# Row-mode steps of two attention stages split into single products, dealt over four row groups, with another queue rule in the planner's model

## The chip, the core and the metric

One core of a Trainium2 chip runs the whole program. The metric is device time in microseconds (us) of one execution, as the median of the runs. The engines are named as in the profile: PE is the matrix engine, DVE the vector engine, ACT the scalar engine, POOL the general one, SP the one that issues most DMAs.

## The reference, cut to what matters

Two layers are applied to `x` of 2 x 2048 tokens with 256 features. Each adds a product of two branches to `x`:

```python
x = L0_attn_x
xn = _layernorm(x, axis=-1)
s = _L0_attn_ref(xn, ...)            # linear attention (elu features), 16 heads of 16
g = _silu(_L0_ffn_ref(xn, ...))      # a block: causal softmax attention, then 8 experts, top 2
x = x + s * g
xn = _layernorm(x, axis=-1)
s = _L1_attn_ref(xn, ...)            # causal softmax attention, 16 heads of 16 + 16
g = _silu(_L1_ffn_ref(xn, ...))      # a product with an int4-rounded matrix, plus a low-rank term
x = x + s * g
```

Both softmax attentions, of 16 heads over 2048 tokens and two batches, are

```python
scores = where(causal, q @ k.T / scale, far below zero)
probs = softmax(scores, axis=-1)
out = probs @ v
```

## The kernel before, in words

The program has three stages: the softmax attention of layer 0 together with the linear attention and the routing of tokens to experts (0 to about 1400 us of the profile), the experts (to about 1930 us), and the softmax attention of layer 1 with everything around it. The change touches the first and the last, which share `run_attention`.

**Groups and rounds.** Heads are handled four at a time, so there are 8 groups (2 batches x 4). A head's queries and keys lie on 32 partitions, so a score product contracts over 32 rows only, and four of them, for the four heads, can stream through PE's four row groups side by side. This is called *row mode* here; in *column mode* (`on="col"`) four products with 32 output columns each run side by side, and in mode *all* one product uses the whole array. `run_attention` makes a list of rounds (`u`). One round holds

- **pass A** of one (query tile `t`, key block `k`): for each of the four heads `j` one product of 128 queries by up to 512 keys (L575), heads 0 and 1 into a pair of PSUM banks, heads 2 and 3 into another; DVE then takes the row maximum of each pair (L594). In layer 0, a block on the diagonal gets a mask first, added by four small bf16 products for each head (`hide`, L534); in layer 1 DVE adds it (L588);
- **pass B** of one (query block `c` of 256, key pair `p`): for each head two products (L609) that give keys by queries into one bank, and ACT's exponential of it (L621). On the diagonal, four bf16 products for each head add the mask (`hide_pair`, L541). In layer 1, one or two bf16 products with three rows subtract the maximum (`less_maximum`, L1697, L1698, L1700); in layer 0 it sits in a spare row of the queries.

Round by round, pass A runs ahead of pass B. With full key blocks, a head has one product of 512 columns and two of 256 in a round. Sums of probabilities with values (L911, L1740) follow in column mode, and projections, transposes, routing and linear attention lie between rounds in modes *all* and *col*.

**The order of the products in a round** is written out by hand. In the loop `for i in (0, 2)` the products come in these groups: A of head 0, B of head 2 (both products), A of head 1, B of head 3; then the masks of A for head 0 (four) and head 1 (four), then those of B for head 2 and head 3; and for `i = 2` the same with A of heads 2 and 3 and B of heads 0 and 1. Each line of this list is one planner step of strand `S`, and PE keeps the order of a strand.

**The planner** (`Plan`) decides the rest: where between the rounds each other step lies on each engine, and which of 8 PSUM banks it takes. `advance` plays the program with costs given in each `S(...)` call, picks the step that can start first (with a handicap for each strand), and `run` searches over jittered handicaps with a beam of 8. Steps of other strands on PE are let in only where the next `S` step opens a round, or where the next `S` step would wait more than `PATIENCE` = 0.3 us longer, mostly for a bank. What the planner sets is only the order of instructions on each engine; the chip then runs each engine's list with semaphores. In the model before, a row step may be sent 0.01 us after the one before it, however many are still waiting for the same group, and it pays a weight load of `LOAD["row"]` = 0.105 us if its group was idle:

```python
                if s.row:
                    if t > groups[s.on] or st.cold[s.on]:
                        t += s.load
                    st.cold[s.on] = False
...
                done, free["PE"] = t + s.cost + self.TAIL - self.GAP, sent + 0.01
```

An f32 product is two records in the trace, each with a weight load (LDWEIGHTS) and a matmul; a bf16 product is one.

Of the kernel before, what the change touches and what calls it, by code (L numbers as in the profile page):

```python
# [17 lines left out]
P = 128  # L18
# [76 lines left out]
class State:  # L95


    def __init__(self, plan):
        self.main = next(iter(plan.queues.get(("S", "PE"), ())), None)
        self.can = {k: q[0] for k, q in plan.queues.items() if not q[0].before}  # L100
        self.waits = [s.before + (s is not plan.queues[s.key][0]) for s in plan.steps]
        self.ready = [0.0] * len(plan.steps)
        self.slot = [None] * len(plan.bufs)
        self.left = [b.uses for b in plan.bufs]
        self.until = [0.0] * len(plan.bufs)
        self.guest = [None] * len(plan.bufs)
        self.since = {k: [0.0] * (plan.BANKS if k == "s" else len(x)) for k, x in plan.kinds.items()}
        self.free, self.groups, self.cold = {}, [0.0] * 4, [True] * 4
        self.mode, self.used, self.held = None, 0.0, {}
        self.todo, self.done, self.value = len(plan.steps), [], 0.0  # L110

# [9 lines left out]
class Plan:  # L121
# [100 lines left out]

    def advance(self, st, handicaps, until):

        free, groups, can, ready = st.free, st.groups, st.can, st.ready
        while st.todo:
            best = shut = None
            low = low_shut = 1e30
# [2 lines left out]
            for key, s in can.items():  # L231
                strand, eng = key
                t = ready[s.n]
                x = free.get(eng, 0.0)
                if x > t:
                    t = x
                busy, closed = t, False
                if eng == "PE":
                    closed = strand != "S" and not (gap and st.used + s.cost <= self.LIMIT)
                    x = top if s.kind != st.mode else groups[s.on] if s.row else top - self.MODE  # L240
                    if x > busy:
                        busy = x
                later = 0.0 if closed else handicaps.get(strand, 0.0)
                if busy + later >= (low_shut if closed else low):
                    continue
                take = ()
                if any(st.slot[b.n] is None for b in s.bufs):
                    found = self.places(st, strand, s, t)
                    if not found:
                        continue  # L250
                    t, take = found
                    if t > busy:
                        busy = t
                if closed:
                    if busy < low_shut:
                        low_shut, shut = busy, (busy, busy, key, s, take, t)
                elif busy + later < low:
                    low = busy + later
                    best = (low, busy, key, s, take, t)
# [4 lines left out]
            _, t, key, s, take, sent = best  # L264
# [18 lines left out]
            done = t + s.cost  # L283
            free[s.eng] = done - min(self.OVERLAP.get(s.eng, 0.0), 0.7 * s.cost)
            worth = self.WORTH[s.eng] * s.cost
            if s.eng == "PE":
                st.used = st.used + s.cost if key[0] != "S" else 0.0
                kind = s.kind
                if kind != st.mode:
                    if kind == "row":  # L290
                        groups[:] = [max(t, x) for x in groups]
                    st.cold[:] = [True] * 4
                if s.row:
                    if t > groups[s.on] or st.cold[s.on]:
                        t += s.load
                    st.cold[s.on] = False
                elif t > max(groups) or st.cold[0]:
                    t += s.load
                    st.cold[0] = False
                done, free["PE"] = t + s.cost + self.TAIL - self.GAP, sent + 0.01  # L300
                if kind == "row":
                    st.mode, groups[s.on] = "row", t + s.cost
                    worth /= 4
                else:
                    st.mode, groups[:] = s.on, [t + s.cost] * 4
            elif s.eng == "SP":
                free["SP"] = t + 0.06
            st.value += worth
# [69 lines left out]
def kernel(ctx: ExitStack, tc: tile.TileContext, i: dict, out: bass.AP):  # L378
    nc = tc.nc
# [45 lines left out]
    cols = keep.tile([P, 8], F32, name="cols")  # L425
# [31 lines left out]
    QC = 256  # L457


    def t_row(n):  # L460
        return 0.00167 * n
# [62 lines left out]
    LAG = 1  # L524
    SUM_LAG0, SUM_LAG = 1, 2
    PREP_AT = 14
    T_HIDE_A, T_HIDE_B = 0.15, 0.28

    def hide(out, j, mask):

        r = slice(32 * j, 32 * j + 32)
        for q in range(4):
            cols = slice(32 * q, P)
            nc.tensor.matmul(out[:, cols], ident_h[r, q], mask[r, q, cols], start=False, stop=q == 3)  # L534

    def hide_pair(out, j, mask):

        r, v = slice(32 * j, 32 * j + 32), out.rearrange("p (n k) -> p n k", n=2)
        for q in (3, 2, 1, 0):
            cols = slice(0, 32 * q + 32)  # L540
            nc.tensor.matmul(v[:, :, cols], ident_h[r, q], mask[r, q, :, cols], start=False, stop=q == 0)  # L541

    def halves_of(c, p):

# [5 lines left out]
    def run_attention(plan, make, prepare, subtract, sum_keys, finish, last_sum, before=None, others=(), between=False, causal=None):  # L550
# [6 lines left out]
        S = plan.step  # L557
# [10 lines left out]
        def pass_a(g, t, k, i, w, mx, parts):  # L568
# [9 lines left out]
                )  # L578

            def products(x):  # L580
                return S("S", "PE", t_row(w), lambda: score(x), r=[(g.qt, t), *((g.kt, n) for n in keys)], w=[(s, x)], on=i + x)

            def rest():
                for x in range(2) if diagonal and causal is None else ():
                    S("S", "PE", T_HIDE_A, lambda x=x: hide(s.t[:, x, w - P : w], i + x, mask_q), r=[(s, x), "ident_h", "mask_q"], w=[(s, x)], on=i + x)
                if diagonal and causal is not None:
                    for x in range(2):
                        S("A", "DVE", t_dve(w) + 0.07, lambda x=x: nc.vector.tensor_tensor_reduce(  # L588
# [12 lines left out]
        def pass_b(g, c, p, j, pt):  # L601
# [2 lines left out]
            w = P + QC if diagonal else 2 * QC  # L604
            ahead = before is not None and p > 0

            def score():
                for n, (kj, q0, at) in enumerate(halves_of(c, p)):
                    nc.tensor.matmul(  # L609
                        s.t[:, at], g.kt.t[r, kj * P : (kj + 1) * P], g.qt.t[r, QC * c + q0 : QC * (c + 1)],  # L610
                        start=n == 0 and not ahead, stop=n == 1 and not (diagonal or before and not ahead),
                    )

            def rest():
                if before and not ahead:
                    S("S", "PE", 0.25 * t_row(w), before(g, c, j, s, diagonal, False, not diagonal), r=[s, g.mh[c]], w=[s], on=j, load=0.026)
                if diagonal:
                    S("S", "PE", T_HIDE_B, lambda: hide_pair(s.t[:, : 2 * P], j, mask_h), r=[s, "mask_h"], w=[s], on=j)

            def weigh():  # L620
                S("B", "ACT", t_act(w), lambda: nc.scalar.activation(pt.t[:, j, :w], s.t[:, :w], AF.Exp, scale=0.25), r=[s], w=[(pt, j)])  # L621

            reads = [(g.kt, 2 * p), (g.kt, 2 * p + 1), (g.qt, 2 * c), (g.qt, 2 * c + 1)]
            opener = None
            if ahead:
                opener = S("S", "PE", 0.25 * t_row(w), before(g, c, j, s, diagonal, True, False), r=[g.mh[c]], w=[s], on=j, load=0.026)
                reads.append(s)
            step = S("S", "PE", t_row(w), score, r=reads, w=[s], on=j)
            return opener or step, rest, weigh

        for part in prepare(groups[0]):
            part()
# [1 line left out]
        for u in range(at + last_sum + 1):  # L634
# [7 lines left out]
            if b:  # L642
                gb, cb, p = b
                pt = Buf("pt")
            first = None
            for i in (0, 2):


                more = []
                if a:  # L650
                    products, after_a = pass_a(g, t, k, i, wa, mx, parts)
                for x in range(2):
                    if a:
                        plan.pace = products(x)
                        first = first or plan.pace
                    if b:
                        step, rest, weigh = pass_b(gb, cb, p, (i + 2 + x) % 4, pt)
                        first = first or step
                        more.append((rest, weigh))
                if a:  # L660
                    after_a()
                for rest, _ in more:
                    rest()
                for _, weigh in more:
                    weigh()
            for call in late:
                call()
            if first and opens:
# [845 lines left out]
    with ExitStack() as sc:  # L1514
# [176 lines left out]
        def less_maximum(G, c, j, s, diagonal, first, last):  # L1691
            r = slice(32 * j, 32 * j + 3)

            def product():
                m = G.mh[c].t[r]
                if diagonal:
                    nc.tensor.matmul(s.t[:, :P], ones_h[r], m[:, P:], start=first, stop=False)  # L1697
                    nc.tensor.matmul(s.t[:, P : P + QC], ones_h[r], m, start=False, stop=last)  # L1698
                else:
                    nc.tensor.matmul(  # L1700
                        s.t.rearrange("p (n q) -> p n q", n=2), ones_h[r], m[:, None].to_broadcast([3, 2, QC]),
                        start=first, stop=last,
                    )

            return product

        def sum_keys(G, c, pair, last):

# [173 lines left out]
```

## Time and profile before

| | |
|---|---|
| median of 3 runs | 3334.01 us (3331.4 to 3335.59) |
| the profiled execution | 3333.86 us; its span in the trace 3332.1 us |
| granted PE clock, mean | 0.982 |
| PE, DVE, ACT, POOL busy | 3205.3, 2132.9, 1623.4, 1620.8 us |
| row-mode records of L575, L609 | 5120 (2560 products), 9216 (4608 products) |
| mask records of L534, L541 | 2048, 2048 |

The span is 1.8 us shorter than the execution's time, and that time is within 0.2 us of the median, so differences in the trace can be read as differences in the median. The start of a matmul in the trace is when its weights begin to load if its group was idle, so a first product looks longer than the next; ends are modelled. Two records of the same row group that follow each other without a gap show by their starts how long one streams.

### The profile page before, as it was taken

The page shows a single profiled execution, that of the slowest core. Times are in us where ns is not written, and L with a number is a line of the kernel's source. Part 1 is how long each engine was busy: PE and PEld are TensorE (multiplying, and loading weights), DVE is VectorE, ACT ScalarE, POOL GpSimd, SP SyncE. Part 2 cuts the span into 40 slices and gives each one's busy share as a digit, 9 for nine tenths or more (in the row PEclk, how much of TensorE's full clock was granted, in tenths as well). Part 3 has the DMA queues.
Part 4 walks back from the last instruction along what each step waited for, and adds up shares of the span by engine and source line. Part 5 has one row for each costly group of instructions (what it writes and reads, how often), then busy time and mean ns, then how long its engine had stood idle before and what let it go on. Part 6 is the DMA issues. An engine that isn't in the chain of part 4 may idle for free.

```text
span 3332.1 us, 92022 instructions
## 1 busy us (share of the span) xinstructions
PE 3205.3 (96%) x39748; PEld 2271.7 (68%) x39748; DVE 2132.9 (64%) x4250; ACT 1623.4 (49%) x3264; POOL 1620.8 (49%) x2006
## 2 busy tenths in 40 slices
PE   7999999989999999979999989999999999999998
PEld 5677777767777776656666646666766666767775
DVE  5677677667777767641112057787777776777785
ACT  3565555555555555511112155555554555544554
POOL 5442222333233222310000057898987776878887
PEclk9999999999999999989999989999999999999999
DMA  5000000000000010133342131110101001000000
GB/s 198 2 2 2 5 8 8 17 30 26 6 11 5 9 45 13 49 109 115 109 131 94 64 105 43 38 43 29 39 17 33 27 17 40 23 12 23 14 29 24
DMA packets 99742, 134.51 MB, mean 40 GB/s; under 512 B 9461, under 2 KB 76739, under 8 KB 99334
## 3 DMA queue, kind: packets, MB, share of 16 engines
q1 hardware_dynamic: 93190, 114.74, 10.6%
q0 software_dynamic: 6144, 13.88, 1.3%
q8 instruction: 311, 5.10, 0.6%
q14 instruction: 97, 0.79, 0.1%
HBM read 93.75 MB, written 37.75 MB: 39 GB/s over the span
## 4 chain that ended last, share of the span: by engine, by line
PE 50%; DVE 3%; POOL 2%; ACT 1%; issue 1%; DMA 0%; POOLq 0%; another core or an unknown queue 0%; SPq 0%; DVEq 0%; ACTq 0%
PE banks L575 9%; PE banks L609 8%; PE banks L414 8%; PE banks L1740 7%; PE s L1488 7%; PE s L1494 7%; PE banks L1751 2%; PE banks L1700 1%; PE banks L541 1%; PE banks L1698 1%; DVE mx L594 1%; POOL ps L1721 1%; ACT pt L621 1%; POOL ps L1717 0%; POOL ps L1722 0%
## 5 line engine op out<-in xcount | busy, mean ns | idle before, releaser
L621 ACT ACTIVATE pt<-banks 128x512 f32<-128x512 f32 (+1 forms) x2304 | 1160.7, 577 | 721.9 <-PE banks L609 321.3
L594 DVE TENSOR_REDUCE mx<-banks 128x2 f32<-128x1024 f32 (+3 forms) x1024 | 1119.1, 1122 | 337.4 <-PE banks L609 141.7
L575 PE MATMUL banks<-carried,carried 32*128 32x512 f32 (+3 forms) x5120 | 1282.3, 566 | 25.0 <-DVE mx L594 10.5
L609 PE MATMUL banks<-carried,carried 32*128 32x256 f32 (+1 forms) x9216 | 1239.8, 378 | 3.8 <-issue 3.7
L609 PEld LDWEIGHTS banks<-carried,carried 32*128 32x128 f32 x9216 | 972.1, 186 | 42.8 <-issue 15.8
L575 PEld LDWEIGHTS banks<-carried,carried 32*128 32x128 f32 x5120 | 545.3, 185 | 242.3 <-issue 108.6
L1717 POOL TENSOR_TENSOR ps<-pt 128x1024 f32<-128x1024 f32 (+1 forms) x159 | 346.7, 2181 | 113.8 <-ACT pt L621 101.8
L1721 POOL TENSOR_TENSOR ps<-ps,pt 128x1024 f32<-128x1024 f32 x127 | 302.4, 2381 | 69.3 <-ACT pt L621 64.8
L848 POOL TENSOR_TENSOR ra<-raw,rope 128x128 f32<-128x128 f32 x128 | 60.1, 470 | 566.3 <-ACT raw L860 496.1
L1700 PE MATMUL banks<-mh,ones_h 3*128 3x512 bf16 x896 | 272.0, 382 | 7.5 <-ACT mh L1688 3.5
L1722 POOL TENSOR_TENSOR ps<-ps,pt 128x1024 f32<-128x1024 f32 (+1 forms) x127 | 269.1, 2119 | 10.0
L911 PE MATMUL banks<-pt,vt 128*32 128x256 f32 (+1 forms) x4608 | 269.1, 371 | 4.3 <-DVE mx L594 3.0
L1740 PE MATMUL banks<-pt,vt 128*32 128x256 f32 (+1 forms) x4608 | 269.0, 371 | 2.5 <-ACT pt L621 2.5
L1497 DVE TENSOR_TENSOR ye<-s,b 128x256 f32<-128x256 f32 x64 | 27.2, 424 | 380.6 <-PE s L1494 380.6
L588 DVE CUSTOM_DVE_ANT_0 banks<-banks,causal 128x384 f32<-128x384 f32 (+3 forms) x512 | 240.3, 515 | 40.5 <-PE banks L575 25.2
L1489 ACT ACTIVATE hm<-s,b1c 128x512 f32<-128x512 f32 x128 | 87.8, 687 | 347.2 <-PE s L1488 346.0
L1488 PE MATMUL s<-xt,carried 128*128 128x512 f32 x512 | 228.2, 604 | 9.7 <-DVE xt L1421 9.7
L1494 PE MATMUL s<-carried,hm 128*128 128x256 f32 x1024 | 223.6, 379 | 0.0
L1740 PEld LDWEIGHTS banks<-pt,vt 128*32 128x32 f32 x4608 | 135.2, 110 | 129.5 <-ACT pt L621 26.4
L1494 PEld LDWEIGHTS s<-carried,hm 128*128 128x128 f32 x1024 | 194.6, 190 | 33.3 <-issue 7.7
L911 PEld LDWEIGHTS banks<-pt,vt 128*32 128x32 f32 x4608 | 134.0, 109 | 114.4 <-issue 15.7
L1488 PEld LDWEIGHTS s<-xt,carried 128*128 128x128 f32 x512 | 97.4, 193 | 131.2 <-issue 110.2
(276 smaller groups left out, 4166.9 us busy)
## 6 DMA issues: line engine op xcount, KB each, us to landing
carried<-in_L_ffn_W_dram SPq DMA_DIRECT2D x32, 1024.0 KB
gl<-g_dram SPq DMA_DIRECT2D x64, 256.0 KB
slots_in<-zero SPq DMA_DIRECT2D x8, 1024.0 KB
slots_out<-ye SPq DMA_DIRECT2D x16, 512.0 KB
xe<-slots_in SPq DMA_DIRECT2D x15, 512.0 KB
s_dram<-lo SPq DMA_DIRECT2D x16, 256.0 KB
hn<-in_L_attn_x_dram SPq DMA_DIRECT2D x16, 256.0 KB
g_dram<-gs SPq DMA_DIRECT2D x16, 256.0 KB
```

Of the source, the lines that this page charges most:

```text
L575: nc.tensor.matmul(s.t[:, x, :w], g.qt.t[r, t * P : (t + 1) * P], g.kt.t[r, 512 * k : 512 * k + w], start=True, stop=not (diagonal and cau ...
L594: S("A", "DVE", t_dve(2 * w), lambda: nc.vector.tensor_reduce(mx.t[:, t % 2, i : i + 2, k], s.t[:, :, :w], AX.X, ALU.max), r=[(s, 0), (s, ...
L609: nc.tensor.matmul(s.t[:, at], g.kt.t[r, kj * P : (kj + 1) * P], g.qt.t[r, QC * c + q0 : QC * (c + 1)], start=n == 0 and not ahead, stop=n ...
L621: S("B", "ACT", t_act(w), lambda: nc.scalar.activation(pt.t[:, j, :w], s.t[:, :w], AF.Exp, scale=0.25), r=[s], w=[(pt, j)])
L911: nc.tensor.matmul(av.t[32 * j : 32 * j + 32, q0:QC], vts[G.vn][:, kj, j], pt.t[:, j, at], start=n == 0, stop=n == len(tiles) - 1,)
L1488: nc.tensor.matmul(ps, w1[:, k, f * P : (f + 1) * P], xt[:, k], start=k == 0, stop=k == 1)
L1494: nc.tensor.matmul(ps[:, :D], hm[:, f, s * P : (s + 1) * P], w2[:, f], start=f == 0, stop=f == FF // P - 1)
L1700: nc.tensor.matmul(s.t.rearrange("p (n q) -> p n q", n=2), ones_h[r], m[:, None].to_broadcast([3, 2, QC]), start=first, stop=last,)
L1717: nc.gpsimd.tensor_tensor(ps.t[:, :, q0:], pt.t[:, :, same], pt.t[:, :, odd], ALU.add)
L1721: nc.gpsimd.tensor_tensor(ps.t, ps.t, pt.t[:, :, even], ALU.add)
L1722: nc.gpsimd.tensor_tensor(ps.t[:, :, q0:], ps.t[:, :, q0:], pt.t[:, :, odd], ALU.add)
L1740: nc.tensor.matmul(av.t[32 * j : 32 * j + 32, q0:QC], G.vt.t[:, kj, j], pt.t[:, j, at], start=n == 0, stop=False)
```

## The change

The row products of a round become planner steps of their own. For layer 0 each head gets a queue of its products in the order in which they must run (`i = 0` first), and the four queues are merged by the time at which the product before would have begun if every head ran alone: first the first product of each head, then the second of each, and a third only after the place at which its head's second begins. For layer 1 (`if before`) the order of the list above is kept. The mask products run from the narrowest to the widest in layer 0 pass A (before: widest first) and likewise in `hide_pair`. In the model, `began[j]` is when group `j`'s newest product begins, and a row product cannot be sent before that time of its group (so a group's third holds the whole queue); a switch of mode takes `MODE` = 0.1 us from the end of all groups, and weights load beside the running product. Each sent step takes 0.007 us instead of 0.01. The strands that are paced by a round (`prep`, `lin`, `mix`, `gate`) follow its last product, not its last pass A product. Costs of the masks go from 0.15 and 0.28 us for four to single costs (columns by 2400 per us, at least 0.027). The costs and handicaps of everything else are the same.

```diff
@@ Plan.advance
                 if eng == "PE":
+                    if s.row and s.kind == st.mode and began[s.on] > t:
+                        t = busy = began[s.on]
...
-                if kind != st.mode:
-                    if kind == "row":
-                        groups[:] = [max(t, x) for x in groups]
-                    st.cold[:] = [True] * 4
+                if s.kind != st.mode:
+                    sent = max(sent, max(groups) + self.MODE)
+                    st.mode, groups[:], began[:] = s.kind, [sent] * 4, [sent] * 4
                 if s.row:
-                    if t > groups[s.on] or st.cold[s.on]:
-                        t += s.load
-                    st.cold[s.on] = False
...
+                    t = max(groups[s.on], sent + s.load)
+                    began[s.on], groups[s.on] = t, t + s.cost
                     worth /= 4
                 else:
-                    st.mode, groups[:] = s.on, [t + s.cost] * 4
+                    t = max(groups[0], sent + s.load)
+                    began[:], groups[:] = [t] * 4, [t + s.cost] * 4
+                done, free["PE"] = t + s.cost + self.TAIL - self.GAP, sent + 0.007
@@ hide (hide_pair likewise)
-        for q in range(4):
-            cols = slice(32 * q, P)
-            nc.tensor.matmul(out[:, cols], ident_h[r, q], mask[r, q, cols], start=False, stop=q == 3)
+        for q in (3, 2, 1, 0):
+            cols = slice(32 * q, P)
+            parts.append((max(0.027, (P - 32 * q) / 2400), lambda q=q, cols=cols: nc.tensor.matmul(
+                out()[:, cols], ident_h[r, q], mask[r, q, cols], start=False, stop=q == 0
+            )))
+        return parts
@@ run_attention, the round
-            first = None
+            first, queues, after, by_step = None, [[] for _ in range(4)], [], []
             for i in (0, 2):
-                more = []
                 if a:
                     products, after_a = pass_a(g, t, k, i, wa, mx, parts)
-                for x in range(2):
-                    if a:
-                        plan.pace = products(x)
-                        first = first or plan.pace
-                    if b:
-                        step, rest, weigh = pass_b(gb, cb, p, (i + 2 + x) % 4, pt)
-                        first = first or step
-                        more.append((rest, weigh))
-                if a:
-                    after_a()
-                for rest, _ in more:
-                    rest()
-                for _, weigh in more:
-                    weigh()
+                    for x in range(2):
+                        queues[i + x] += products(x)
+                        by_step += [((i, 0, 2 * x), i + x, e) for e in products(x)]
+                    after.append(after_a)
+                for j in ((i + 2) % 4, (i + 3) % 4) if b else ():
+                    products, weigh = pass_b(gb, cb, p, j, pt)
+                    queues[j] += products()
+                    by_step += [((i, e[5], 2 * (j % 2) + 1), j, e) for e in products()]
+                    after.append(weigh)
+            order = []
+            for j, q in enumerate(queues):
+                began, until = -1.0, 0.0
+                for n, entry in enumerate(q):
+                    order.append((began, j, n, entry))
+                    began, until = until, until + entry[0]
+            order.sort(key=lambda x: x[:3])
+            if before:
+                order = [(0, j, 0, entry) for _, j, entry in sorted(by_step, key=lambda x: x[0])]
+            for _, j, _, (cost, fn, r, w_, load, *_) in order:
+                step = S("S", "PE", cost, fn, r=r, w=w_, on=j, load=load)
+                first = first or step
+            if a:
+                plan.pace = step
+            for call in after:
+                call()
```

`pass_a`, `pass_b`, `hide`, `hide_pair` and `less_maximum` now return lists of single products with cost, reads and writes in place of calls that issue several.

## The prediction

> **What bounds the kernel now.** First the page, for the engine that sets the end; then the busy times by stage; then PE's timeline inside single rounds, because a busy share of PE says nothing about its four row groups.
>
> ```profile
> PE 3205.3 (96%) x39748; PEld 2271.7 (68%) x39748; DVE 2132.9 (64%) x4250; ACT 1623.4 (49%) x3264; POOL 1620.8 (49%) x2006
> ...
> PE 50%; DVE 3%; POOL 2%; ACT 1%; issue 1%; DMA 0%; POOLq 0%; another core or an unknown queue 0%; SPq 0%; DVEq 0%; ACTq 0%
> ```
>
> PE is busy for 96% of the span, and the chain that ended last is almost only PE. The stages (the attention stages are the first and third window):
>
> ```profile
> 0.00:1400.00 1400.00, 1350.47 (x17079) 998.75 (x17080) 987.99 (x1872) 782.50 (x1665) 454.55 (x1095) 0.99 0.07 24
> ...
> 1930.00:3332.00 1402.00, 1357.06 (x20750) 943.59 (x20749) 1049.34 (x2109) 730.03 (x1432) 1128.51 (x857) 0.98 0.10 31
> ```
>
> After the window's length come PE, PEld, DVE, ACT and POOL. In layer 0 DVE has 71% and ACT 56%, in layer 1 POOL 80% and DVE 75%. PE sets the pace in both, so time taken out of PE's rounds can leave the span.
>
> Now one plain round of layer 0 (512 keys, no mask; start, duration, records). I write A0 for pass A of head 0, B2 and B2' for the two products of pass B for head 2. The order is A0 B2 B2' A1 B3 B3' A2 B0 B0' A3 B1 B1'.
>
> ```profile
> 453.76 0.69 PE L575 MATMUL banks<-carried,carried 32*128 32x512 f32 x1
> 453.77 0.48 PE L609 MATMUL banks<-carried,carried 32*128 32x256 f32 x1
> 453.78 0.69 PE L575 MATMUL banks<-carried,carried 32*128 32x512 f32 x1
> ...
> 454.30 0.59 PE L575 MATMUL banks<-carried,carried 32*128 32x512 f32 x1
> ...
> 454.74 0.59 PE L575 MATMUL banks<-carried,carried 32*128 32x512 f32 x1
> 454.75 0.47 PE L609 MATMUL banks<-carried,carried 32*128 32x256 f32 x1
> 454.76 0.67 PE L575 MATMUL banks<-carried,carried 32*128 32x512 f32 x1
> 455.17 0.69 PE L575 MATMUL banks<-carried,carried 32*128 32x512 f32 x2
> ...
> 455.80 0.33 PE L871 MATMUL banks<-cst,pad 128*128 128x128 f32 x1
> ```
>
> A2's two records start at 454.74 and 455.17: 512 columns stream for 0.43 us a record, 0.86 a product, so 256 columns take 0.43. A0's records lie 0.54 apart (453.76, 454.30): starting cold costs 0.10. Each group has 0.86 + 2 x 0.43 = 1.72 us of streaming; with 0.10 to start, and 0.10 from the last stream's end to the next mode, that is 1.93. The round took 455.80 - 453.76 = 2.03. The rest is in B1 (454.75, 0.47 long where a warm one is 0.37) and A3 (454.76, 0.67 for 0.59): both start cold although their groups had been streaming until that moment. Ahead of them stands B0', the third of group 0: A0 streams until 454.73 and B0 waits behind it. So B0' holds PE's queue, A3 and B1 behind it come too late to load their weights beside the running product, and two groups lose 0.08 to 0.10. The holding rule of the changed model is thus visible before the change.
>
> With masks it costs more. This round began at 540.53, with A of 512 and B both on the diagonal:
>
> ```profile
> 541.09 0.38 PE L609 MATMUL banks<-carried,carried 32*128 32x128 f32 x3
> 541.49 0.23 PE L534 MATMUL banks<-mask_q,ident_h 32*128 32x128 bf16 x2
> 541.52 0.29 PE L541 MATMUL banks<-mask_h,ident_h 32*128 32x256 bf16 x2
> ...
> 541.73 0.48 PE L609 MATMUL banks<-carried,carried 32*128 32x256 f32 x1
> ...
> 543.16 0.33 PE L937 MATMUL banks<-cst,un 128*128 128x128 f32 x1
> ```
>
> B2' and B3' stop streaming near 541.3, but their masks (L541) start at 541.52: A0's masks stand in front, wait for A0 to end at 541.49, and hold the queue. Then group 0 waits for its B0 until the masks of heads 2 and 3 have passed (541.73, cold again). The round takes 2.63 us, for 1.94 of streaming in a group (A 0.86, its masks 0.14, B 0.65, its masks 0.29 at the rate seen here with four groups at once).
>
> **Layer 0, the deal.** All 6656 row products stay, with the same columns. The order becomes A0 A1 B2 B3, B0 B1 B2' B3', A2 A3, B0' B1'. A2, third of group 2, now holds only things that are needed later. Laying each kind of round out in its new order with these stream times, the 0.10 for a cold start, 0.10 at the end, and the hold by a third product and taking the old length as the median of that kind's rounds in the trace (laid out in the same way, the old plain round comes to 2.04, the doubly masked one to 2.76 against 2.63, so some new lengths may be 0.1 too long):
>
> - A 512 plain with B plain: 148 rounds, 2.03 to 1.93: 14 us.
> - A 512 masked with B masked: 25 rounds, 2.63 to 2.16: 12.
> - A plain with B masked: 24, 2.10 to 1.99: 3.
> - A masked (384, 256, 128, 512) with B plain: 24 x 0.08, 21 x 0.15, 17 x 0.25, 7 x 0.21: 11. For 256 and 128 the trace shows more (2.09 and 1.82), but part of that is waiting for banks, which stays.
> - A masked (128, 384) with B masked: 7 x 0.59 and 7 x 0.25: 6.
> - A masked alone: 11 x 0.56 (1.34 to 0.78), 8 x 0.36: 9. A plain alone: none.
> - B alone: 8 rounds, 3.
>
> Together 58 us of the 700 that layer 0's row bursts take (67 by the difference of the two layouts).
>
> A page reads against this. The Trainium skill, "TensorE: Matmul & The Clock Gate", Part 3, "The mechanism", gives PE a 64-deep window that pulls weight loads for another row group ahead, with matmuls starting strictly in program order. By the first half, A3 and B1 could never be cold and the deal would be worth 0; by the second, A1 (453.78) could not have started before B2', which is ahead of it and streams only after B2. This trace shows both otherwise.
>
> **What the deal costs.** B0 and B1 move from behind A2 (PE gets there some 0.4 us into the round) to places 5 and 6, so their banks are claimed 0.4 us earlier, and a late one holds B2', B3', A2 and A3. Pairing each bank's first product with its reader in the trace: at 280 starts of rounds, 185 had no older A or B bank unread, a fifth had more than two; the time until only two were left, cut at 0.4, averages 0.06 us. Times 288 rounds with B: 17 us at most, 0 if the planner puts other work there. I take 10, nearer the upper end because faster rounds leave DVE and ACT less time. The compiled order shows the planner doing just that: bursts that end after two of four heads go from 39 to 78, changes between modes in layer 0 from 723 to 758. A change costs 0.10 us, five more row bursts (337 to 342) 0.10 of load each: 4 us.
>
> The rest of the edit issues no new DMA, semaphore or DVE, ACT and POOL instruction; the maxima and exponentials follow the same products. Reversing the masks' widths changes no sum of columns. Pacing by the last product only moves places in the order: nothing, or a few tenths hidden behind the 2 us between bursts.
>
> **Layer 1.** The compiled order of its row products is the same product by product, so the holds stay. Only the places between change, chosen by a model that now knows the holds: row bursts 252 to 235, mode changes 517 to 485: 32 x 0.10 + 17 x 0.10 = 5 us gained. Its 250 bursts in the trace take 754 us; the streams (541), 0.2 for each burst (50) and the holds, laid out as above (about 100), make 690, so some 64 us are waits for other engines. A better placed order could take two fifths of them (25); handicaps chosen with the other model could add a third (20). I take a gain of 6, near the middle.
>
> **The sum.** -58 + 10 + 4 - 5 - 6 = -55 us, on the profiled execution's 3333.86, which is the median within 0.2: 3279. Low end: no bank waits and layer 1 at its best, -58 + 4 - 5 - 25, is -84; by the two layouts' 67 in place of 58 it is -93, and 3243 lies between. High end: half of the deal's gain is given back to DVE and ACT, all 17 of bank waits, nothing more in layer 1: -29 + 17 + 4 - 5 = -13, 3320.
>
> **The rivals.**
> *Slower: the early claim.* B0's bank, in place 5, holds four groups. Its price is up to 0.4 us in each of 288 rounds, 115 us, and with the other terms (-65) the time is 3384. It decides from 65/288 = 0.23 us a round. For it: some 20 more broken rounds in the order. Against it: two thirds of the rounds start with no old bank unread.
> *Given back.* The maximum (L594, 1.12 us mean, two in a round) and ACT's exponentials free the banks; if they set the pace, PE's 58 us turn into waits and some 15 remain: 3319. Against it: DVE would rise only from 71% to 74% of the stage. The Trainium skill, "TensorEngine Tiling (Array Packing)", "PSUM Bottleneck", warns that emptying PSUM may become the limit once tiling speeds PE up; by it this would be the likeliest case, with 3319. The stage's row does not show that limit.
> *It does nothing.* If what I read as a hold is only late banks, the order does not matter: 3334, less about 1 for mode changes. Against it: 126 plain rounds standing alone have a median of 2.031 and a minimum of 2.030; late banks would scatter.
>
> **How the numbers follow.** Forecast 0.70 (own range 3250 to 3310), still better in both layers 0.06 (3235), given back 0.14, nothing 0.04, the early claim 0.06. About 0.2%, 6.7 us, is what a measurement here tells from no change: faster takes the first two and 0.11 of the third, 0.87; same 0.03 + 0.03 = 0.06; slower 0.06 + 0.01 = 0.07. From 3243 to 3320 leaves out half of the second, the early claim, and some of the rest: under 2 in 10.
>
> **What would show it.** After the change the plain round should last 1.93 us, with no first record of A2, A3, B0 or B1 longer than 0.60 or 0.38; the doubly masked one 2.16; layer 0's row bursts 650 us together; the experts should start about 44 us earlier, and the third stage be about 11 us shorter. It is wrong if plain rounds stay at 2.03 (no hold), if the fifth product waits for ACT's semaphore (the early claim), or if PE's idle time behind L594 and L621 grows by as much as the rounds shrink (given back).

## The result, and the profile after

The changed kernel takes 3425.45 us (median of 4 runs, 3424.04 to 3430.99), the kernel before beside it 3334.8 (4 runs): a ratio of 1.0276, 95% interval 1.0258 to 1.0294. It is slower by 2.8%, where 3279 was forecast. In the changed kernel the lines are: pass A L575, pass B L610, masks L527 and L537, maximum L596, exponential L635, sums L927 and L1756.

The page's busy times and its chain, then the first and third stage as before:

```profile
PE 3256.4 (95%) x39748; PEld 2220.5 (65%) x39748; DVE 2134.7 (62%) x4250; ACT 1622.5 (47%) x3264; POOL 1613.7 (47%) x2006
...
PE 83%; DVE 7%; POOL 3%; ACT 3%; issue 2%; DMA 1%; another core or an unknown queue 0%; SPq 0%; DVEq 0%; POOLq 0%; ACTq 0%
```

```profile
0.00:1400.00 1400.00, 1312.10 (x16328) 893.27 (x16328) 942.40 (x1756) 743.63 (x1588) 433.87 (x1070) 0.99 0.07 23
...
1930.00:3332.00 1402.00, 1368.52 (x19944) 944.72 (x19943) 1005.09 (x2031) 702.36 (x1371) 1064.99 (x826) 0.99 0.11 33
```

In the same 1400 us PE runs 16328 records, before 17079, and it is busy for 38 us less; DVE falls from 71% to 67%, ACT from 56% to 53%. So DVE and ACT have not become the bound: PE, DVE and ACT are all busy for less of the time. (The shares of the two chains are not compared: those of before add up to 57% of the span, these to 99%.) By stages of the two profiled executions the experts start at 1527.7 us (before 1446.2, so layer 0 lost 81.5), they last 470.7 (before 470.9), and layer 1 takes 1425.6 (before 1409.7, so 15.9 lost). Together that is 97 us of span; most of the loss is in layer 0. Its row bursts (unbroken runs of row products, up to the next product of another mode) grew by 56 us, from 702.1 to 758.1; the other 25 lie between them.

Now a plain round of layer 0 in the changed kernel, with the engines that read it (lines of weight loads and of one other tile left out):

```profile
433.13 0.70 PE L575 MATMUL banks<-carried,carried 32*128 32x512 f32 x2
433.15 0.70 PE L610 MATMUL banks<-carried,carried 32*128 32x256 f32 x4
433.67 0.59 PE L575 MATMUL banks<-carried,carried 32*128 32x512 f32 x2
433.68 0.79 PE L610 MATMUL banks<-carried,carried 32*128 32x256 f32 x6
434.11 0.59 PE L575 MATMUL banks<-carried,carried 32*128 32x512 f32 x2
434.31 2.36 DVE L596 TENSOR_REDUCE mx<-banks 128x2 f32<-128x1024 f32 x2 [0.56 <-PE banks L610]
434.31 0.60 PE L610 MATMUL banks<-carried,carried 32*128 32x256 f32 x4
434.54 0.59 PE L575 MATMUL banks<-carried,carried 32*128 32x512 f32 x2
434.74 0.38 PE L610 MATMUL banks<-carried,carried 32*128 32x256 f32 x2
434.76 2.06 ACT L635 ACTIVATE pt<-banks 128x512 f32<-128x512 f32 x4 [1.72 <-PE banks L610]
435.41 0.66 PE L416 MATMUL banks<-cst,xr 128*128 128x128 f32 x4 [0.27 <-ACT pt L635]
```

Every record after the first of its group streams warm: A2 and A3 both have their first record at 434.11 and their second at 434.54, 0.43 apart and 0.59 long, and the last streams end near 434.97, 1.84 us after the start. Before, they took 1.94. So the hold is gone, as forecast. But look at ACT. Its first exponential reads B2 and B2'. A2, next in their row group, starts at 434.11, so B2' was through by then; the exponential starts at 434.76. In PE's order B0 and B1 stand ahead of B2' and B3'. They are second in groups 0 and 1, behind the 512 columns of A0 and A1, and stream until 434.53 (the single records: second ones at 434.31, the next of their groups at 434.53). The exponential starts 0.23 us after that. The maximum, whose A0 and A1 stand first, starts 0.2 after they end. Then PE is idle: the rows end at 434.97, and the next product (L416) waits for ACT until 435.41. The round takes 2.28 us; most took 2.33.

In the plain round of before that the prediction shows (from 453.76), both readers started 1.24 us after the round:

```profile
455.00 2.36 DVE L594 TENSOR_REDUCE mx<-banks 128x2 f32<-128x1024 f32 x2 [0.67 <-PE banks L609]
455.00 1.58 ACT L621 ACTIVATE pt<-banks 128x512 f32<-128x512 f32 x3 [1.36 <-issue]
```

The packed trace also keeps the times at which PE's semaphore rises, by which readers learn that a product has ended. Of the first eight products of the changed round only A1, B2' and B3' raise it, B0 and B1 don't. It rises at 434.29, 434.73 and 434.78. So B2', through by 434.11, was told at 434.73, 0.20 us after the streams of B0 and B1.

**Theory 1.** The end of a product reaches other engines in the order of PE's list, whatever the row group. **Rivals.** (2) The new model and the plan it draws cost the time, not the order. (3) B0 and B1, now in places 5 and 6, claim banks too early (the prediction's rival).

Medians over layer 0, start of the first exponential and of the two maxima after the round's start: plain rounds had 1.25 and 1.24, 2.38, now 1.68 and 1.18, 2.34. In rounds with both blocks masked, A0's masks stand behind A2 and A3 in the new order, and there it is the maximum that comes late: 1.34, 2.59 before, 2.25, 3.39 now. One such round of the changed kernel, from 917.47:

```profile
917.47 0.70 PE L575 MATMUL banks<-carried,carried 32*128 32x512 f32 x2
...
918.53 0.30 PE L527 MATMUL banks<-mask_q,ident_h 32*128 32x128 bf16 x2
...
918.95 0.59 PE L575 MATMUL banks<-carried,carried 32*128 32x512 f32 x2
...
919.38 0.17 PE L527 MATMUL banks<-mask_q,ident_h 32*128 32x32 bf16 x1
...
919.66 1.23 DVE L596 TENSOR_REDUCE mx<-banks 128x2 f32<-128x1024 f32 x1 [1.59 <-PE banks L527]
919.76 0.64 PE L927 MATMUL banks<-pt,vt 128*32 128x256 f32 x8
```

The widest masks of A0 and A1 (L527, 128 columns) start at 918.53 and 918.62 and are short; the maximum of A0 and A1 still waits until 919.66. A2 and A3, ahead of those masks in the list, stream until 919.38, and the semaphore that tells of the masks rises at 919.63.

What that does to PE, in the waits of weight loads between 80 and 1330 us (total, times, longest): before

```profile
PEld banks L575 <- DVE mx L594: 25.6, 58, 3.4
...
PEld banks L911 <- ACT pt L621: 12.8, 41, 0.4
...
PEld banks L841 <- ACT pt L621: 11.2, 34, 0.4
```

and after

```profile
PEld banks L575 <- DVE mx L596: 31.8, 67, 1.1
PEld banks L927 <- ACT pt L635: 27.9, 52, 3.3
PEld banks L857 <- ACT pt L635: 25.3, 38, 2.1
...
PEld banks L575 <- ACT pt L635: 17.2, 34, 1.6
```

The sums (L911, now L927) and the projections (L841, now L857) wait for the exponentials more than twice as long as before: the banks that they and the next round need come free late.

### The profile page after: what moved, and what is told of

Same layout as the page of the kernel before. It is cut to its first block, busy times and chain, and to the rows that moved or that the text cites. A ratio compares the mean times of both kernels' runs of the same rounds, so it can differ in the third digit from the quotient of the medians.

```text
span 3429.2 us, 92049 instructions
## 1 busy us (share of the span) xinstructions
PE 3256.4 (95%) x39748; PEld 2220.5 (65%) x39748; DVE 2134.7 (62%) x4250; ACT 1622.5 (47%) x3264; POOL 1613.7 (47%) x2006
## 4 chain that ended last, share of the span: by engine, by line
PE 83%; DVE 7%; POOL 3%; ACT 3%; issue 2%; DMA 1%; another core or an unknown queue 0%; SPq 0%; DVEq 0%; POOLq 0%; ACTq 0%
PE banks L575 17%; PE banks L610 15%; PE banks L409 7%; PE banks L927 7%; PE s L1504 7%; PE s L1510 6%; PE banks L1756 6%; DVE mx L596 3%; ACT pt L635 3%; PE banks L857 2%; PE banks L537 2%; PE banks L1189 2%; PE banks L1767 2%; PE banks L416 2%; POOL ps L1737 1%
## 5 line engine op out<-in xcount | busy, mean ns | idle before, releaser
L635 ACT ACTIVATE pt<-banks 128x512 f32<-128x512 f32 (+1 forms) x2304 | 1157.9, 577 | 813.2 <-PE banks L610 379.2
L596 DVE TENSOR_REDUCE mx<-banks 128x2 f32<-128x1024 f32 (+3 forms) x1024 | 1116.9, 1121 | 373.0 <-PE banks L575 160.9
L575 PE MATMUL banks<-carried,carried 32*128 32x512 f32 (+3 forms) x5120 | 1271.6, 562 | 34.4 <-DVE mx L596 14.2
L610 PE MATMUL banks<-carried,carried 32*128 32x256 f32 (+1 forms) x9216 | 1221.5, 380 | 3.2 <-issue 1.6
L610 PEld LDWEIGHTS banks<-carried,carried 32*128 32x128 f32 x9216 | 919.4, 187 | 80.2 <-issue 28.4
L575 PEld LDWEIGHTS banks<-carried,carried 32*128 32x128 f32 x5120 | 530.6, 185 | 254.5 <-issue 109.8
L927 PE MATMUL banks<-pt,vt 128*32 128x256 f32 (+1 forms) x4608 | 273.2, 375 | 6.7 <-ACT pt L635 6.2
L1756 PE MATMUL banks<-pt,vt 128*32 128x256 f32 (+1 forms) x4608 | 272.0, 375 | 2.2 <-ACT pt L635 2.1
L1756 PEld LDWEIGHTS banks<-pt,vt 128*32 128x32 f32 x4608 | 136.2, 110 | 133.0 <-ACT pt L635 30.7
L927 PEld LDWEIGHTS banks<-pt,vt 128*32 128x32 f32 x4608 | 134.8, 110 | 132.1 <-ACT pt L635 30.0
```

The lines of the kernel that those rows point to most:

```text
L575: nc.tensor.matmul(s.t[:, x, :w], g.qt.t[r, t * P : (t + 1) * P], g.kt.t[r, 512 * k : 512 * k + w], start=True, stop=not (diagonal and cau ...
L596: S("A", "DVE", t_dve(2 * w), lambda: nc.vector.tensor_reduce(mx.t[:, t % 2, i : i + 2, k], s.t[:, :, :w], AX.X, ALU.max), r=[(s, 0), (s, ...
L610: nc.tensor.matmul(s.t[:, at], g.kt.t[r, kj * P : (kj + 1) * P], g.qt.t[r, QC * c + q0 : QC * (c + 1)], start=n == 0 and not ahead, stop=n ...
L927: nc.tensor.matmul(av.t[32 * j : 32 * j + 32, q0:QC], vts[G.vn][:, kj, j], pt.t[:, j, at], start=n == 0, stop=n == len(tiles) - 1,)
L1756: nc.tensor.matmul(av.t[32 * j : 32 * j + 32, q0:QC], G.vt.t[:, kj, j], pt.t[:, j, at], start=n == 0, stop=False)
```

## The experiments

The experiments came in three sets. The kernels of one set ran on one chip beside the kernel before, which took 3332.24, 3284.9 and 3352.63 us in the three sets. So ratios to it are compared, not times across sets. Of each trace I took the layer-0 rounds that stand unbroken and the start of the engines' work in them.

**First set: four kernels, of which three missed their aim.** `f1` and `f2` keep the kernel before and its plan, and were to write the plain rounds' products in another order within the same places: `f1` as dealt, `f2` with B2', B3' ahead of B0, B1.

```diff
+DEALT = [A0, A1, B2, B3, B0, B1, B2', B3', A2, A3, B0', B1']    # f1, in short
+DEALT = [A0, A1, B2, B3, B2', B3', B0, B1, A2, A3, B0', B1']    # f2
```

> The kernel before, with its plan and its model untouched; only in layer 0's plain rounds (512 keys, no mask, not broken by other work; 126 in the trace of before) the products are put on PE in the order of the change: A0 A1 B2 B3 B0 B1 B2' B3' A2 A3 B0' B1'. Theory 1 (a product's end is told to the other engines only when everything ahead of it in PE's order has ended): B0 and B1, which stream until 1.40 us after the round's start, now stand ahead of B2' and B3', which end at 0.99; so the first exponential starts near 1.68 us after the round's start instead of 1.25, the row products themselves still end 0.1 us earlier, and what follows waits for ACT: slower by 20 to 40 us (126 x 0.2 to 0.3). Rival 2 (the deal is good, the new model's places cost the time): faster by 10 to 13 us. Rival 3 (the early claim of the banks of B0 and B1): slower, with B0 or B1 starting late inside the round.

> As the run with the changed order in the plan of before, but with the plain rounds in the order A0 A1 B2 B3 B2' B3' B0 B1 A2 A3 B0' B1': only B0, B1 and B2', B3' change places, no group's third comes earlier. Theory 1: the exponentials start at 1.2 us after the round's start, the streams end 0.1 us earlier than before, nothing is told late: faster than before by 5 to 13 us. Rival 2: the same gain here, but then also in the run with the changed order. Rival 3: as slow as the run with the changed order, since the banks of B0 and B1 are claimed as early within 0.02 us.

1.0018 [1.0006, 1.003] and 1.0007 [0.9995, 1.002]. Neither tells anything about the order: readers lie between a round's steps in the plan, so almost no round was rewritten (the first exponential is still at 1.25 us in `f1`). They show the scatter instead: layer 1, with the same order, took 1409.7 us in the profile of before, 1415.2 in `f1` and 1420.9 in `f2`.

`e1` is the changed kernel with its products in the list's order also in layer 0, `e3` the changed kernel sorted by when a product would end instead of begin.

```diff
-            if before:
+            if True:                                          # e1
...
-                    order.append((began, j, n, entry))
+                    order.append((until, began, j, n, entry))  # e3
```

> The changed kernel with layer 0's products in the old list order (the condition that keeps it for layer 1 now holds for both); the new model, the single steps and the narrowest-first masks stay. Theory 1: layer 0 loses the whole of its 81 us (experts start at 1440 to 1460 us), layer 1 stays as in the changed kernel: 3335 to 3355. Rival 2: layer 0 stays long, 3400 or more. Rival 3: as theory 1.

> The changed kernel with the four queues of layer 0 merged by each product's own end if every head ran alone, not by the start of the one before it; model and single steps as in the changed kernel. Plain rounds become B2 B3 A0 A1 B2' B3' B0 B1 A2 A3 B0' B1'; masks of A stand ahead of the third products again. Theory 1: exponentials and maxima are told on time, 60 us or more faster than the changed kernel, 3290 to 3365, the masked rounds giving back part of the deal's gain by holds. Rival 2: 3400 or more. Rival 3: near 3425, the banks of B0 and B1 are claimed as early.

`e1`: 1.1065 [1.0997, 1.1134]. It wasn't the old order: each A product's masks came directly behind it and, waiting for it, held PE's queue. Layer 0 took 1786.5 us, its row bursts 984.8 (before 702.1), though plain rounds handed over their exponentials at 1.25 as before. That is the hold at its dearest, but not alone: the granted clock averaged 0.91 in this layer 0 (before 0.98), so part of the 340 us may be the clock. `e3`: 1.034 [1.0319, 1.0361], where I had forecast a kernel 60 us faster than the changed one. Its plain rounds are on time (1.29), its doubly masked ones are not: first exponential 1.86, maxima at 2.04 and 4.19. The experts start at 1538.9 us. So late masked rounds are enough for a loss of this size, which theory 1 allows but this run doesn't prove.

**Second set: the order alone, and the model alone.** `g1` and `g2` are `f1` and `f2` with readers inside a round moved behind it where that is allowed: 132 of the 148 plain rounds are rewritten, everything else stays in the plan of before. `e5` is the changed kernel (single steps, new model) in the true old order of the list. `e7` is the changed kernel in which no product of `i = 2` comes ahead of one of `i = 0` in rounds that have both passes:

```diff
-                    order.append((began, j, n, entry))
+                    order.append((entry[-1] if a and b else 0, began, j, n, entry))   # i first
```

> As the first run with the plan of before, where nearly no round met the condition; now 132 of the 148 plain rounds of layer 0 put their products on PE in the changed order, together at the place of the round's last step, and all other engines keep their lists. Theory 1 (an end is told in PE's order): first exponential 1.6 to 1.7 us after the round's start instead of 1.25, streams 0.1 us shorter, slower than before by 15 to 40 us. Rival 2 (the new model's places cost the time): 10 to 13 us faster.

> The same 132 rounds with A0 A1 B2 B3 B2' B3' B0 B1 A2 A3 B0' B1'. Theory 1: exponentials at 1.2 us, streams 0.1 us shorter, 5 to 13 us faster than before. Rival 2: the same gain, but then in its sister run too. Rival 3 (early claim of banks): as slow as its sister.

> The changed kernel with the old list order in layer 0, masks behind the products of both heads as before (in the earlier run with this aim each head's masks came directly behind its product of pass A, and held the queue). The new model and the narrowest-first masks stay. Theory 1: maxima and exponentials are told as before, layer 0 within 15 us of before, 3330 to 3360. Rival 2: 3400 or more.

> The changed kernel, but in rounds with both passes of layer 0 no product of the second half (i = 2) stands ahead of one of the first half; inside a half the deal is that of the change. Plain rounds: A0 A1 B2 B3 B2' B3' A2 A3 B0 B1 B0' B1'. Laid out with the hold and with ends told in PE's order, the streams end as early as in the changed order (1.85, masked 2.09), and first maxima and exponentials are told at 0.97 to 1.11 us in all kinds instead of up to 1.92. Theory 1: layer 0 30 to 60 us shorter than before, 3280 to 3320 in all. Rival 2: 3400 or more. Rival 3: near 3425, as B0 and B1 claim their banks in places 9 and 10, within 0.6 us of the round's start, partly better.

| | ratio to before | first exponential, plain rounds | unbroken plain rounds: number, median, shortest | experts start, us | layer 1, us |
|---|---|---|---|---|---|
| `g1`, dealt | 1.0136 [1.011, 1.0161] | 1.68 | 126, 2.333, 2.254 | 1452.0 | 1400.6 |
| `g2`, B2' B3' first | 0.9998 [0.9987, 1.001] | 1.31 | 126, 1.986, 1.934 | 1404.4 | 1400.2 |
| `e5`, old order | 1.0021 [1.0008, 1.0035] | 1.25 | 133, 2.031, 2.030 | 1409.4 | 1407.5 |
| `e7`, half by half | 1.0067 [1.0041, 1.0092] | 1.31 | 89, 1.980, 1.933 | 1422.8 | 1405.8 |

One plain round of `g1`, then the same of `g2` (in both kernels L638 is pass A, L677 pass B, L660 the maximum, L689 the exponential):

```profile
441.13 0.70 PE L638 MATMUL banks<-carried,carried 32*128 32x512 f32 x2
...
442.31 2.36 DVE L660 TENSOR_REDUCE mx<-banks 128x2 f32<-128x1024 f32 x2 [0.54 <-PE banks L638]
...
442.82 1.57 ACT L689 ACTIVATE pt<-banks 128x512 f32<-128x512 f32 x3 [2.13 <-PE banks L677]
...
443.46 0.92 PE L913 MATMUL banks<-wqkv,ht 128*128 128x192 f32 x4
```

```profile
429.50 0.70 PE L638 MATMUL banks<-carried,carried 32*128 32x512 f32 x2
...
430.67 2.36 DVE L660 TENSOR_REDUCE mx<-banks 128x2 f32<-128x1024 f32 x2 [0.54 <-PE banks L677]
...
430.81 1.57 ACT L689 ACTIVATE pt<-banks 128x512 f32<-128x512 f32 x3 [1.79 <-PE banks L677]
...
431.46 0.92 PE L913 MATMUL banks<-wqkv,ht 128*128 128x192 f32 x4
```

The maximum comes 1.18 and 1.17 us after the start, the exponential 1.69 and 1.31, the next product 2.33 and 1.96. In a list of twelve, two neighbouring pairs (places 5 to 8) have changed places. `g1` loses 3329.35 - 3284.9 = 44.5 us (forecast 15 to 40) with the plan, the model and the masked rounds of before: rival 2 can't explain that. By theory 1, 0.30 us a round (2.333 for 2.031) in 132 rounds make 40. `g2` gives 46 us back.

The semaphore says the same over all unbroken plain rounds. In the changed kernel B2' and B3' are through 0.99 us after the round's start, in the median, and the first of them is told at 1.60; in `g2` they are through at 0.99 too and the first is told at 1.23. The exponential starts 0.08 us later in both.

Rival 3 is there, but not as the price. In `g1` B0 or B1 came late for a bank in most rounds: A2 starts later than 1.05 us in 110 of 126 (0.98 if nothing waits), by 0.25 in the median. Yet the 16 rounds of `g1` without that delay have the same medians, 1.68 for the exponential and 2.33 for the round, and so have the 67 of 93 in the changed kernel. The delay lies under the wait for ACT. `g2` bounds what it costs by itself: there B0 and B1 also stand ahead of A2, their banks are claimed as early within 0.02 us, and A2 is late in 27 of 126 rounds, which take 2.30 in the median where the others take 1.96. By these figures that is some 9 us if all of it comes from the early claim, and `g2` still equals the kernel before.

`e5` clears most of the model's name: with single steps and the new model but the old order, 0.2% is lost, about what layer 1 differs by (1407.5 for 1400.6). `e7` differs from the changed kernel in a sort key and takes its 2.8% down to 0.7%. But I had expected it below before, and `g2` too, by the shorter rounds. Their shortest plain rounds are the 1.93 of the forecast; in `g2` the gain of 0.045 in the median, 126 times, is under 6 us, and the interval leaves room for about 4. In `e7` fewer rounds stand unbroken: 59 of the 148 plain ones are cut by other work, in `e5` 15, before 22.

**Third set: whose are the broken rounds?** `e2` is the changed kernel with the model of before (its `advance` and `State`). `e6` is the changed kernel and `e8` is `e7` with a model that knows ends are told in order:

```diff
-                done, free["PE"] = t + s.cost + self.TAIL - self.GAP, sent + 0.007
+                done, free["PE"] = max(t + s.cost + self.TAIL - self.GAP, st.told), sent + 0.007
+                st.told = done
```

`e4` is the kernel before with another seed for the planner's draws.

> The changed kernel's single products in the dealt order, placed by the kernel before's model (no row held by a group's third product, mode changes not priced). Theory 1 (the end of a product is told in the order of the list, so the dealt list hands ACT its inputs late): the model has no part in the loss, plain rounds' first exponential starts 1.6 to 1.8 us after the round as in the changed kernel, and the time is 1.02 to 1.035 of before. Rival (the loss is the plan that the new model draws): within 0.5% of before, 0.995 to 1.005.

> The changed kernel, with one thing more in its model: a product's end counts no earlier than that of the product ahead of it in TensorE's order. The dealt order itself stays. Theory 1: the inputs still come late (first exponential of a plain round at 1.6 to 1.8 us), the planner can only fill the wait better: 1.010 to 1.028 of before. Rival (the late inputs cost only because the planner did not know of them): 1.000 to 1.006, as with the old order of the list.

> The half-by-half order (no product of the second pair of heads' pass A or its pass-B partners ahead of the first pair's) with the model that counts ends in TensorE's order. If the remaining 0.7% of the half-by-half run came from rounds that the planner broke because it counted on ends told early, it goes: 0.993 to 1.003 of before, bursts of row products in layer 0 back from 359 towards 320. Rival (the row products' 0.1 us is worth nothing because the banks turn over at the pace of ACT and VectorE, and the breaks are the planner's scatter): 1.003 to 1.010.

> The kernel before, with another seed for the planner's draws and nothing else: measures how far the time moves between two plans of the same program. If differences of half a per cent between plans are scatter, it lands within 0.995 to 1.008 of before; if the plan is worth more than that, beyond.

| | ratio to before | first exponential, plain rounds | unbroken plain rounds of 148 | experts start, us | layer 1, us |
|---|---|---|---|---|---|
| `e2`, dealt, old model | 1.0208 [1.0191, 1.0225] | 1.68 | 100 | 1534.3 | 1412.7 |
| `e6`, dealt, told in order | 1.0195 [1.0178, 1.0212] | 1.68 | 79 | 1504.2 | 1433.1 |
| `e8`, half by half, told in order | 1.0116 [1.0099, 1.0133] | 1.31 | 91 | 1474.8 | 1436.1 |
| `e4`, other seed | 1.0006 [0.9996, 1.0016] | 1.25 | 130 | 1448.6 | 1429.1 |

`e2`: without the new model 2.1% are lost, and layer 1 shows none of it (1412.7 us, where the profile of before has 1409.7 on a chip 0.6% faster). That rules rival 2 out as the main cause a second time. Where the rest of the changed kernel's 2.8% lies is not shown: its layer 1 took 1425.6 us and that of `e2` 1412.7, but two plans differ by as much (`e4`). `e6`: a planner that knows of the late ends saves some layer-0 time, but the exponentials stay at 1.68 and the loss at 2%. `e8` went against me: I had put `e7`'s broken rounds down to a planner that counts on early ends, but with that mended 57 rounds are still broken (`e7` 59), and the ratio is worse (above both forecasts, and the intervals don't meet). `e4`: another plan of the same program lies within 0.2% of before in total, though its layer 1 took 16 us more than `e2`'s, which has the same model. Layer 1 alone is not told apart by less than that.

**What stays open.** Every dealt list that the planner placed has 48 to 69 broken plain rounds, under three models; the old list has 15 to 22, and `e1`, with the masks moved, 43. The planner lets other work in where the next row step would wait over 0.3 us for a bank, and the dealt lists claim banks in another order. That this is what breaks them, and that the breaks are `e7`'s 0.7%, was not tested. No version here beat the kernel before; `g2` equals it.

## Why the prediction was wrong

*The hold: right.* Rounds lost time to a third product holding PE's queue. Without it, plain rounds took 1.933 us at the shortest in `e7` and 1.934 in `g2`, for a forecast of 1.93, and in the changed kernel the rows' streams end 0.1 us earlier. The doubly masked round fell from 2.63 to 2.29, not to 2.16. "It does nothing" is refuted. But that the shorter streams save time in all is not shown: `g2`, which has them, equals the kernel before.

*The step that failed* is in "What the deal costs": "the maxima and exponentials follow the same products". They follow the same products, but they are told of a product's end only when all products ahead of it in PE's list have ended. The deal put B0 and B1, whose groups were busy until 0.97 us, ahead of B2', which was through at 0.98, and the first exponential went from 1.25 to 1.68 us. The layout counted when streams end. With ends told in the order of the list and 0.2 us to the reader, it gives 1.60 and 2.12 for the first exponential of a plain round and the first maximum of a doubly masked one; measured 1.68 and 2.25. The plain round, forecast at 1.93, has a median of 2.333, and layer 0's row bursts last 758.1 us (before 702.1, forecast 650). The term of -58 for the deal came out as a loss of 81.5 in the profiled layer 0; plain rounds alone make 44.5 of such a loss (`g1`). Other kinds lost too: unbroken rounds with a plain A and a masked B went from 2.10 to 2.30, those with a masked A of 256 keys and a plain B from 2.09 to 2.40.

*The page on the clock gate.* The Trainium skill, "TensorE: Matmul & The Clock Gate", Part 3, "The mechanism", says that matmuls keep program order in their starts and in their ends. The prediction took up only the starts, and set the page aside because A1 started before B2'. For starts the trace does stand against it: over different row groups they don't follow the list. But I let ends run free as well, and there this case agrees with the page in what readers see: ends are told in program order, B2' at 1.60 us instead of 1.23. On the weight loads pulled ahead, the trace still stands against it in these rounds: the old plain rounds stay at 2.03 in `e5`, and reordering removes 0.1 of their streams.

*The early claim* had "slower" right, but not by its mechanism, so that was luck. Waits of that kind are in the trace of `g1`, but under the longer wait for ACT. In `g2`, where nothing is told late, they make some 9 us at most, which leaves room for most of my 10 but not for the 115 of the rival.

*Given back* was right in where PE would wait (behind L596 and L635) and wrong in why: DVE and ACT are less busy in the stage than before, not more. They are not at their limit but get their inputs late.

*Layer 1*, forecast 11 us shorter, took 15.9 longer in the profile, and in the second set about 7 longer under the new model (`e5`) than under the old plan (`g1`). Fewer row bursts (252 to 235) bought nothing that shows. A gain is not there; whether there is a loss is not shown, as two plans of one model differ by as much (`e2` and `e4`, 16 us).

*The range* reached 3320 because all of its bad ends were gains that shrink. The one case for slower was a wait of PE; that the readers of PE could be told late was not among the cases.

## What to carry to other kernels

Before reordering work on one engine, lay out two times for every instruction: when it ends, and when everything ahead of it in the list has ended; on PE the readers went by the second here. Put whatever another engine waits for ahead of work that is merely able to start, above all ahead of work that queues behind something long. Try a new order with the rest of the plan held still (`g1` and `g2` differ in one exchange of two pairs, and by 1.4%); a scheduler that draws a new plan mixes the order's effect with its own.

## What the runs showed of the hardware

- PE's row groups run ahead of one another, but ends are told in list order: B2' was through at 0.98 us of the round, its reader started at 1.63 to 1.69 while B0 and B1 stood ahead of it, and at 1.31 with the two swapped. In the doubly masked round A0's masks were through near 918.67, and the maximum started at 919.66, 0.28 after A3's end. PE's semaphore shows the same: the first of B2' and B3' was told at 1.60 us in the changed kernel and at 1.23 in `g2` (medians), 0.61 and 0.24 after they were through.
- A product whose row group still has two f32 products before it holds PE's queue for all four groups. Taking the third out of the way shortens a plain round's streams from 1.94 to 1.84 us; masks that wait directly behind their own product (`e1`) made layer 0 about 340 us longer, at a granted clock of 0.91 for 0.98.
